# Graph attention on one core: q of two tiles by seven half-width products, with the bias laid into the PSUM bank

## The chip, the cores and the metric

The kernel runs on one core of a Trainium2 chip. The metric is the device time of one execution in microseconds; before the change it is 1974.93 us, the median of three runs (1974.34 to 1975.01). The profile is of one further execution, with a span of 1981.3 us and a granted TensorE clock of 0.990. Engines are named as in the profile: PE is TensorE, PEld its weight loads, DVE VectorE, ACT ScalarE, POOL GpSimd, SP SyncE.

## The reference

The input x is 16 batches of 1024 rows of 512 numbers, and adj a 1024 x 1024 matrix of zeros and ones, sparse and denser towards its first rows and columns. All is fp32.

```python
q = (x @ Wq + bq).reshape(b, n, 8, 64)
k = (x @ Wk + bk).reshape(b, n, 8, 64)
v = (x @ Wv + bv).reshape(b, n, 8, 64)
scores = jnp.einsum('bqhd,bkhd->bhqk', q, k) / jnp.sqrt(64.)
scores = scores + (1.0 - adj) * -1000000000.0
attn = softmax(scores)
out = jnp.einsum('bhqk,bkhd->bqhd', attn, v).reshape(b, n, 512) @ Wo + bo
result = layernorm(x + out)
```

## The kernel before

The kernel makes lists of the neighbours from adj once (DVE, in the first 200 us). Then it does two things at a time. The "fronts" transpose x and compute q, k and v, two tiles of 128 rows (a pair) at a time, and store them in DRAM. The "blocks" gather rows of q, k and v by the lists (POOL), multiply and sum them to scores (DVE), take exponentials and weigh v (ACT, part DVE), and add up (DVE, PE). A finished tile goes through the output projection (po) and the norm. The program is emitted in steps, one for each of 560 blocks and a lead-in of 34: in each step the engines get a block's work, and PE gets units of front or output work for a share of time in credit. What a unit leaves in PSUM is emptied in the next step (`later(1, ...)`).

PSUM has eight banks: a ring of four for short-lived results, one each for x and z, two for sums.

```python
def fill_psum(name):
    return psum.tile([P, HALF], F32, tag="fill", name=name, bufs=4)
```

k and v of a pair come from seven products of blocks (two rows of tiles times k and v together), with weights combined once at the start (T1 to T4) and x combined per pair (s1 to s4). q is computed plainly, four products of 128x128x512 for each tile, and gets scale and bias when DVE takes it out of its bank:

```python
def product(name, lhs, w, out):
    def unit(c):
        if c == 0:
            PS[name] = fill_psum(name)
        p = PS[name]
        nc.tensor.matmul(p, lhs()[:, ts(c, P)], w[:, c, :], start=(c == 0), stop=(c == NPAIR - 1))
        if c == NPAIR - 1:
            del PS[name]
            later(1, lambda: out(p))
    return [(PRODUCT, lambda c=c: unit(c), None) for c in range(NPAIR)]
# ... in pair(b, j):
def out_q(i, p):
    q = work.tile([P, D], F32, tag="q", name=f"q_{b}_{tt[i]}", bufs=2)
    nc.vector.scalar_tensor_tensor(q, p, scale, bq_bc, op0=OP.mult, op1=OP.add)
    later(1, lambda: nc.sync.dma_start(q_rows[b % ROWS][ds(tt[i] * P, P), :], q))
# ...
units = []
units += unit("x", lambda: a(0, 0), B11, True, out_e, None)
units += unit("p6", s(2), T2, True, out_w, None)
units += q0
units += unit("x", lambda: a(0, 1), B21, False, lambda: out_k(0, R["x"]), "e")
units += unit("p7", s(3), T3, True, out_g, None)
units += xt
units += unit("z", s(1), T1, True, out_v1, None)
units += q1
units += unit("p4", lambda: a(1, 1), T4, True, out_k1, None)
units += unit("z", s(4), B22, False, out_v0, "v1")
```

A unit of k and v is two products of 128x128x512. Units p6, p7 and p4, the products of q and po, and the transposes pxT (of x) and poT (of an attention result) each take a bank of the ring of four; x and z have their own.

The transposes of x, and the combinations of two tiles after them:

```python
def out():
    XT[b, t] = work.tile([P, D], F32, tag="xT", name=f"xT_{b}_{t}", bufs=4)
    nc.scalar.copy(XT[b, t], p)
    # ...
    if t % 2 and (b, t) != (0, 1):
        later(1, combine)

def combine():
    s = [work.tile([P, HD2], F32, tag=f"s{i}", name=f"s{i}_{b}_{t}", bufs=1 + i // 4) for i in (1, 2, 3, 4)]
    x0, x1 = XT[b, t - 1], XT[b, t]
    nc.vector.tensor_tensor(s[0], x1[:, 0:HD2], x1[:, HD2:D], op=OP.add)
    # ... three more of 128x256
```

The exponential, and the order in a step (cut):

```python
nc.scalar.activation(PV[n][:, D:], S.pop(n), AF.Exp, bias=bias)
# ... a step n:
exponentials(n + 3)              # ACT
products(n + 4)                  # DVE: qk
gather(...)                      # POOL, up to AHEAD = 8 blocks ahead (AHEAD_LAST = 11 without fronts)
weigh(n + 1)                     # DVE, for some blocks
add_own(n); scores(n + 4)        # DVE
normalise(...)                   # DVE, at the end of a tile
for fn in plan.pop(n, ()): fn()  # what later(...) has put off: PSUM is emptied here
weigh(n + 2)                     # ACT, eight of 128x64, for most blocks
for fn in rest.pop(n, ()): fn()
add_up(n)                        # PE, for blocks of a list
# ... then units of PE, until the credit of this step is used up
```

## Time and profile before

| what | value |
|---|---|
| time, median of 3 runs | 1974.93 us |
| span of the profiled execution | 1981.3 us |
| PE busy | 1914.7 us (97%) |
| DVE busy | 1786.6 us (90%) |
| ACT busy | 1554.5 us (78%) |
| products that read wq (q), 1024 records | 481.5 us |
| DVE taking q out of PSUM, 128 operations of 128x512 | 87.2 us |
| 16 DMA engines, mean | 284 GB/s |

Busy time is the time in which an engine has at least one instruction under way. The rows of instructions that follow each other overlap, so the mean length of one is more than the time it takes of its engine; the distance from start to start is that time. A matmul in fp32 shows as two records. "Idle before" a group is what the engine waited ahead of it, and the releaser is what ended the wait.

### The profile page before, as it was taken

Reading aid. Unit: us, or ns where it says so; the run is one execution under the profiler, and the core shown is the slowest. Engines: PE = TensorE matmul, PEld = TensorE weight load, DVE = VectorE, ACT = ScalarE, POOL = GpSimd, SP = SyncE. Lnnn points to the kernel's source line nnn. Section 1 sums busy time; section 2 is a strip of 40 time slices with the busy share of each in tenths; the row PEclk is TensorE's granted clock in tenths of the full one; section 3 lists DMA queues with packets and bytes.
Section 4 is the critical chain, followed back from the end, with each engine's and each line's share of the span. In section 5 each row is a group of like instructions: output and inputs, shape, how many; then the busy total and the mean of one; then the engine's idle time right before and its main releaser. Section 6 shows DMA issues by size and latency. Waiting matters only on the chain.

```text
span 1981.3 us, 25750 instructions
## 1 busy us (share of the span) xinstructions
PE 1914.7 (97%) x5375; PEld 923.3 (47%) x5375; DVE 1786.6 (90%) x3756; ACT 1554.5 (78%) x6096; POOL 1288.2 (65%) x1206
## 2 busy tenths in 40 slices
PE   8988999999999999999999999999999999999895
PEld 3434454444545454454544445454444545444442
DVE  2789999999899999999998999989899999999895
ACT  3525878878797887879888787879789798978785
POOL 1653565756667676767667586766757675566684
PEclk9999999999999999999999999999999999999998
DMA  6697887888879788888889788888978889998994
GB/s 250 214 339 253 265 303 246 301 280 273 315 262 318 253 303 287 299 296 270 306 255 319 269 290 285 298 303 262 312 260 290 293 291 321 313 316 269 324 313 154
DMA packets 191140, 563.10 MB, mean 284 GB/s; under 512 B 31711, under 2 KB 31739, under 8 KB 190974
## 3 DMA queue, kind: packets, MB, share of 16 engines
q0 software_dynamic: 121632, 403.22, 61.9%
q1 hardware_dynamic: 66736, 153.16, 20.9%
q10 hardware_dynamic: 2606, 4.99, 0.7%
q14 instruction: 122, 1.00, 0.2%
q8 instruction: 44, 0.72, 0.1%
HBM read 442.25 MB, written 143.71 MB: 296 GB/s over the span
## 4 chain that ended last, share of the span: by engine, by line
PE 75%; DVE 12%; issue 3%; ACT 2%; DMA 0%; POOL 0%; another core or an unknown queue 0%; DVEq 0%; POOLq 0%; ACTq 0%
PE po L584 19%; PE pq L584 17%; PE pp L698 13%; PE z L698 9%; PE x L698 9%; DVE qk L931 3%; DVE s L935 2%; PE poT L1008 2%; PE pxT L555 2%; PE sum L981 2%; PE sum L980 2%; ACT pv L955 1%; DVE pv L971 1%; PE pm L646 1%; DVE o L1000 1%
## 5 line engine op out<-in xcount | busy, mean ns | idle before, releaser
L910 POOL DMA_INDIRECT kvg<-kv_rows,key_row x560 | 629.5, 1124 | 435.0 <-ACT pv L945 111.6
L955 ACT ACTIVATE pv<-kvg,pv 128x64 f32<-128x64 f32 x3552 | 894.4, 338 | 0.0
L584 PE MATMUL pq<-wq,xT 128*128 128x512 f32 x1024 | 481.5, 600 | 2.0 <-issue 1.5
L584 PE MATMUL po<-wo,oT 128*128 128x512 f32 x944 | 436.7, 595 | 4.2 <-DVE y L804 1.9
L935 DVE TENSOR_REDUCE s<-qk 128x8 f32<-128x512 f32 x560 | 380.8, 680 | 6.0
L931 DVE TENSOR_TENSOR qk<-qt,kvg 128x512 f32<-128x512 f32 x464 | 317.4, 684 | 4.8 <-DMA kvg<-kv_rows,key_row 3.1
L584 PEld LDWEIGHTS pq<-wq,xT 128*128 128x128 f32 x1024 | 192.7, 193 | 223.2 <-issue 209.4
L584 PEld LDWEIGHTS po<-wo,oT 128*128 128x128 f32 x944 | 175.5, 191 | 206.1 <-issue 190.8
L698 PE MATMUL pp<-t,s 128*128 128x512 f32 x504 | 239.6, 598 | 9.5 <-DVE s L570 9.5
L698 PE MATMUL x<-b,xT 128*128 128x512 f32 x504 | 237.1, 593 | 0.0
L971 DVE TENSOR_TENSOR pv<-pv,pv 128x520 f32<-128x520 f32 x336 | 232.9, 693 | 0.0
L945 ACT ACTIVATE pv<-s,absent 128x8 f32<-128x8 f32 x464 | 135.3, 293 | 107.7 <-DVE s L935 69.2
L830 POOL DMA_INDIRECT out_dram<-y,asked_row x128 | 153.2, 1197 | 37.6 <-issue 26.1
L894 POOL DMA_INDIRECT qt<-q_rows,asked_row x128 | 139.8, 1092 | 36.8 <-issue 35.0
L594 ACT ACTIVATE sq_k<-kv 128x128 f32<-128x128 f32 x512 | 150.6, 299 | 10.0 <-DVE kv L721 9.0
L698 PEld LDWEIGHTS pp<-t,s 128*128 128x128 f32 x504 | 95.2, 191 | 119.1 <-issue 107.7
L698 PEld LDWEIGHTS x<-b,xT 128*128 128x128 f32 x504 | 94.6, 190 | 112.4 <-issue 109.0
L752 POOL DMA_INDIRECT y<-in_x_dram,asked_row x102 | 116.0, 1137 | 30.6 <-issue 30.0
L904 POOL DMA_INDIRECT qg<-q_rows,query_row x96 | 106.1, 1105 | 27.2 <-issue 25.3
L698 PE MATMUL z<-b,s 128*128 128x512 f32 x252 | 118.5, 592 | 0.7 <-DVE kv L726 0.7
L698 PE MATMUL pp<-t,xT 128*128 128x512 f32 x252 | 118.5, 593 | 0.1
L698 PE MATMUL z<-t,s 128*128 128x512 f32 x252 | 118.6, 593 | 0.0
(195 smaller groups left out, 2608.8 us busy)
## 6 DMA issues: line engine op xcount, KB each, us to landing
kv_rows<-kv SPq DMA_DIRECT2D x128, 512.0 KB
x<-in_x_dram SPq DMA_DIRECT2D x128, 256.0 KB
q_rows<-q SPq DMA_DIRECT2D x128, 256.0 KB
kvg<-kv_rows,key_row POOLq DMA_INDIRECT x560
residual<-y_sorted SPq DMA_DIRECT2D x26, 256.0 KB
y<-residual SPq DMA_DIRECT2D x26, 256.0 KB
adj<-in_adj_dram POOLq DMA_DIRECT2D x8, 512.0 KB
spill<-oT SPq DMA_DIRECT2D x10, 256.0 KB
```

The lines of the kernel that those rows point to most:

```text
L584: nc.tensor.matmul(p, lhs()[:, ts(c, P)], w[:, c, :], start=(c == 0), stop=(c == NPAIR - 1))
L594: nc.scalar.activation(sq, s[:, ts(h, P)], AF.Square, scale=scale, accum_out=sums[:, h:h + 1])
L698: nc.tensor.matmul(R[bank], l[:, ts(c, P)], right[:, c, :], start=(first and c == 0), stop=(c == 1), skip_group_check=True,)
L752: nc.gpsimd.indirect_dma_start(out=y, out_offset=None, in_=x_rows, in_offset=bass.IndirectOffsetOnAxis(ap=asked_row[:, t:t + 1], axis=0), ...
L830: nc.gpsimd.indirect_dma_start(out=out_rows[b, t], out_offset=bass.IndirectOffsetOnAxis(ap=asked_row[:, t:t + 1], axis=0), in_=y, in_offse ...
L894: nc.gpsimd.indirect_dma_start(out=QT[b, t], out_offset=None, in_=q_rows[b % ROWS], in_offset=bass.IndirectOffsetOnAxis(ap=asked_row[:, t: ...
L910: nc.gpsimd.indirect_dma_start(out=KG[n], out_offset=None, in_=kv_rows[b % ROWS], in_offset=bass.IndirectOffsetOnAxis(ap=key_row[:, g:g + ...
L931: nc.vector.tensor_tensor(QK[n], q, KG[n][:, 0:D], op=OP.mult)
L935: nc.vector.tensor_reduce(S[n], QK.pop(n).rearrange("p (h d) -> p h d", d=HD), axis=AX.X, op=OP.add)
L945: nc.scalar.activation(PV[n][:, D:], S.pop(n), AF.Exp, bias=bias)
L955: nc.scalar.activation(pv[:, ts(h, HD)], v[:, ds(D + h * HD, HD)], AF.Copy, scale=pv[:, D + h:D + h + 1])
L971: nc.vector.tensor_tensor(PV[b, t], PV[b, t], pv, op=OP.add)
```

## The change

q of a pair is now computed by seven block products instead of eight, in the same scheme as k and v: the two tiles are the block rows, the halves of the 512 numbers the block columns, and Wq is taken as four blocks A11, A12, A21, A22 of 256x256. One product of blocks is two products of 128x128x256. It uses the combinations s1 to s4 of x that k and v have already, and combinations U1 to U4 of Wq made once at the start (U1 in the place of A12). It is for TensorE: a pair has fourteen half-width products in place of eight full ones.

A bank of PSUM of its own ("xq") holds the two halves of the sums. ACT fills it with the bias ahead of a pair (`prefill`), and the products add to that; the bias of the right half is stored as a difference to the left. The ring "fill" goes from four banks to three for it. Three products (q6, q7, q4) go to banks of the ring. DVE adds the parts in five operations of 128x256, ACT copies two.

The scale leaves q and its bias and goes into the exponential. To make room in SBUF, the rings of y and kv lose a buffer each. The lists at the start are begun a step apart (`EDGES_FROM`), with more PE work beside them (`LISTS_SHARE`); the sorting of residuals moves by three steps, and the look-ahead of gathers in the last stretch (`AHEAD_LAST`) falls from 11 to 9. The combinations of x for the next pair wait until the product that reads s1 has been issued.

```diff
-KG_BUFS, Q_BUFS, PV_BUFS, Y_BUFS = 8, 7, 5, 6
+KG_BUFS, Q_BUFS, PV_BUFS, Y_BUFS = 8, 7, 5, 5
-SORTED_AT = range(-16, -3)
-AHEAD_LAST = 11
+SORTED_AT = range(-13, 0)
+AHEAD_LAST = 9
-EDGES_FROM = (-17, -16, -15, -13, -11, -8, -7, -18)
+EDGES_FROM = (-17, -16, -15, -14, -13, -12, -11, -18)
-LISTS_SHARE = 4.6
+LISTS_SHARE = 5.4
@@
-            return psum.tile([P, HALF], F32, tag="fill", name=name, bufs=4)
+            return psum.tile([P, HALF], F32, tag="fill", name=name, bufs=3)
@@
+        A11, A12, A21, A22 = (W["q"][:, ts(i, 2), ts(j, HD2)] for i in range(2) for j in range(2))
+        U2, U3, U4 = (one.tile([P, 2, HD2], F32, name=name) for name in ("u2", "u3", "u4"))
+        U1, mixed = A12, [False]
@@ combine
+                    if (b, t) != (0, 3) and last_s.get((b * NT + t) // 2 - 1) is None:
+                        later(1, combine)
+                        return
@@ pair
+            L, RIGHT = slice(0, HD2), slice(HD2, D)
+            def prefill():
+                R["xq"] = q_psum(f"xq_{b}_{j}")
+                nc.scalar.copy(R["xq"], bq_bc)
+            def q_unit(bank, left, right, after, need=None):
+                def pe():
+                    if bank in (L, RIGHT):
+                        out, first = R["xq"][:, bank], False
+                    else:
+                        R[bank] = out = fill_psum(f"{bank}_{b}_{j}")[:, L]
+                        first = True
+                    l = left()
+                    for c in range(2):
+                        nc.tensor.matmul(
+                            out, l[:, ts(c, P)], right[:, c, :], start=(first and c == 0), stop=(c == 1),
+                            skip_group_check=True,
+                        )
+                    later(1, after)
+            # q_e, q_11: ACT copies of 128x256; q_w, q_g, q_22, q_21, q_12: DVE adds of 128x256
             units = []
             units += unit("x", lambda: a(0, 0), B11, True, out_e, None)
+            units += [(0.0, prefill, lambda: mixed[0] and before_this in q_done)]
             units += unit("p6", s(2), T2, True, out_w, None)
-            units += q0
+            units += q_unit(L, lambda: a(0, 0), A11, q_e)
             units += unit("x", lambda: a(0, 1), B21, False, lambda: out_k(0, R["x"]), "e")
+            units += q_unit("q6", s(2), U2, q_w, "qe")
             units += unit("p7", s(3), T3, True, out_g, None)
+            units += q_unit(L, lambda: a(0, 1), A21, q_11, "qe")
             units += xt
             units += unit("z", s(1), T1, True, out_v1, None)
-            units += q1
+            units += q_unit("q7", s(3), U3, q_g)
+            units += q_unit(RIGHT, s(1), U1, q_22)
             units += unit("p4", lambda: a(1, 1), T4, True, out_k1, None)
+            units += q_unit("q4", lambda: a(1, 1), U4, q_21, "q22")
             units += unit("z", s(4), B22, False, out_v0, "v1")
+            units += q_unit(RIGHT, s(4), A22, q_12, "q22")
@@ gather, without fronts: kv ring of 4 instead of 5; load_y: at most 4 tiles instead of 5
@@ exponentials
-            nc.scalar.activation(PV[n][:, D:], S.pop(n), AF.Exp, bias=bias)
+            nc.scalar.activation(PV[n][:, D:], S.pop(n), AF.Exp, bias=bias, scale=scale)
```

## The prediction

> **What bounds the kernel now.** I read the page's busy shares first, then the same busy times cut into stretches, then the groups by shape, and last the timelines. The page says that TensorE (PE) is busy nearly throughout:
>
> ```profile
> PE 1914.7 (97%) x5375; PEld 923.3 (47%) x5375; DVE 1786.6 (90%) x3756; ACT 1554.5 (78%) x6096; POOL 1288.2 (65%) x1206
> ```
>
> A share over the whole span mixes stages, so here is the busy time by stretch (from, to, length; then PE, weight loads, DVE, ACT and POOL busy in us, and the PE clock). The first three lines are of one cut, the last is of a finer one:
>
> ```profile
> 300.00:1600.00 1300.00, 1294.15 (x3671) 627.72 (x3671) 1213.78 (x2491) 1078.57 (x4288) 898.42 (x826) 1.00 0.85 286
> ...
> 0.00:200.00 200.00, 177.58 (x477) 82.80 (x478) 140.14 (x347) 89.82 (x290) 84.33 (x98) 0.97 0.77 265
> 1700.00:1982.00 282.00, 243.64 (x666) 116.00 (x665) 245.86 (x552) 220.07 (x843) 181.13 (x167) 0.95 0.81 280
> ```
>
> ```profile
> 1700.00:1800.00 100.00, 90.86 (x260) 43.80 (x260) 98.14 (x185) 85.45 (x358) 60.99 (x55) 0.98 0.89 306
> ```
>
> From 300 to 1600 us PE is busy for 1294 of 1300 us. PE alone sets that time, with DVE close behind at 93.4% and ACT at 83%. From 1700 on it is DVE that is full (98.1%) and PE waits. So a saving of PE time counts before about 1700 us, and not after.
>
> The chain that ended last gives the same picture (PE 75% of it). The list of waits names what PE itself waited for, in us in total, times, and the longest:
>
> ```profile
> PE poT L1008 <- DVE o L1000: 10.6, 7, 3.2
> PE pp L698 <- DVE s L570: 9.5, 3, 4.0
> ...
> PE po L584 <- DVE y L804: 1.9, 1, 1.9
> PE po L584 <- DVE g L717: 1.2, 2, 1.0
> ```
>
> The last two are waits for a PSUM bank of the "fill" ring to be emptied. There are hardly any with four banks.
>
> **What an instruction costs.** A busy PE or DVE row overlaps the next one, so I take the pitch, start to start. The PE timeline:
>
> ```profile
> 361.25 2.74 PE L584 MATMUL po<-wo,oT 128*128 128x512 f32 x6
> 363.82 0.59 PE L980 MATMUL sum<-pv,sums 128*128 128x256 f32 x2
> 364.26 0.61 PE L981 MATMUL sum<-pv,sums 128*128 128x264 f32 x2
> 364.70 1.02 PE L584 MATMUL po<-wo,oT 128*128 128x512 f32 x2
> 365.56 3.60 PE L584 MATMUL pq<-wq,xT 128*128 128x512 f32 x8
> 368.99 1.88 PE L698 MATMUL x<-b,xT 128*128 128x512 f32 x4
> ```
>
> Each product is two records. Four 128x128x512 products take 368.99 - 365.56 = 3.43 us, so one takes 0.858. A 256-wide one takes 364.26 - 363.82 = 0.44, half of that: narrow products lose next to nothing in this kernel. The DVE timeline:
>
> ```profile
> 361.35 0.69 DVE L959 TENSOR_TENSOR pv<-kvg,pv 128x512 f32<-128x512 f32 x1
> 361.95 0.69 DVE L971 TENSOR_TENSOR pv<-pv,pv 128x520 f32<-128x520 f32 x1
> ...
> 382.00 0.42 DVE L568 TENSOR_TENSOR s<-xT 128x256 f32<-128x256 f32 x1
> 382.33 0.42 DVE L569 TENSOR_TENSOR s<-xT,xT 128x256 f32<-128x256 f32 x1
> 382.67 0.42 DVE L570 TENSOR_TENSOR s<-s,xT 128x256 f32<-128x256 f32 x1
> ```
>
> A 512-wide operation has a pitch of 0.60 us, a 256-wide one 0.33 to 0.34. On ACT, two 512-wide copies out of PSUM at 380.74 let the next instruction start at 381.68, so 0.47 to 0.48 each.
>
> **What the Trainium skill says.** (1) "TensorE: Matmul & The Clock Gate", section "Back-to-back issue gap": the spacing of matmuls is set by the weight load and the matmul together. The trace agrees that this doesn't bite yet: a load lasts 0.19 us, a 256-wide record streams for 0.215. The margin is thin, as the new products have no 512-wide neighbours in a run of four records. (2) "Perfetto Trace Analysis", section "Optimizing Scalar/DVE Operations": each DVE or ACT operation carries an overhead of its own, and part of its profiled latency overlaps the next. The trace agrees: 0.68 us long at a pitch of 0.60, and two halves of 0.34 cost more than one whole. (3) The same page, section "Matmuls": independent groups should rotate through PSUM banks so that emptying one overlaps the next group. The change takes one bank out of that rotation. (4) "PSUM — Partial Sum Buffer", section "PSUM bank collisions raise a hardware error": two engines may not be in one bank at once, even at different columns. Both halves of q now share one bank, so emptying one half excludes writing the other. Nothing in the trace before shows this.
>
> **The change part by part.** Counting the records that read wq by stretch and dividing by 16 (two tiles, four products, two records) gives the pairs of tiles: 11.6 before 300 us (one of them plain, which stays as it is), 43.7 from 300 to 1600, 4.1 from 1600 to 1700, 4.9 after. A pair in the middle takes 1300 / 43.7 = 29.7 us.
>
> PE: eight 512-wide products, 8 x 0.858 = 6.86 us a pair, become fourteen 256-wide ones, 14 x 0.43 = 6.01. It saves 0.86 us a pair. For 63 pairs that is 54 us; the 58.4 pairs before 1700 give 50, and this is the most that can arrive.
>
> DVE: out go two 512-wide operations (2 x 0.60 = 1.20), in come five 256-wide ones (5 x 0.34 = 1.70): 0.50 us more a pair. From 300 to 1600 that is 22 us, on 1213.8: 1235.7. PE falls there to 1294 - 37.5 = 1256.7. So DVE would stand at 1235.7 / 1262.5 = 97.9%, as full as it was at its fullest (98.1%). The 4.9 pairs after 1700 cost 2.5 us more, as DVE sets the time there.
>
> ACT: a 512-wide fill of the bank with the bias (0.48) and two 256-wide copies (0.28 each, an estimate between the 0.25 pitch of its 128x64 operations and 0.48) are 1.04 us a pair. ACT goes to (1078.6 + 45) / 1262.5 = 89%. It executes in order, and eight weighing operations (2.0 us) stand ahead of the fill in most steps. PE has one x and one p6 unit, 3.4 us, to cover the way from the last read of the bank, over the fill, to the next product.
>
> The scale in the exponential and the unscaled bias cost nothing: the exponential already runs, with one more constant. The smaller y and kv rings and the shorter look-ahead of the last stretch free the memory for the new weight combinations; I allow no time for them beyond the width of the range. The lists brought together and the larger share of PE work beside them can win back a little of the 22 us that PE idles before 200 us; I put 3.
>
> Banks: per batch of four pairs the fill ring serves 4 x 7 + 16 = 44 allocations before and 4 x 8 + 16 = 48 after. A bank may be held 4 x 119 / 44 = 10.8 us on average before, and 3 x 115 / 48 = 7.2 after. In the timeline a pq bank begun at 1026.27 is read at 1030.48 and free at 1031.2 (4.9 us), so the mean suffices, but not bursts: at 1024.1 a po bank (begun 1019.8, free at 1025.7), a poT bank and two pxT banks are held at once. With three, the second pxT would have waited until 1025.7, some 1.5 us.
>
> The sum: -50 (PE before 1700) + 2.5 (DVE after) - 3 (start) + L, where L is what PE loses to banks, to the bias fill and to a DVE without slack. For L I choose 0.35 us a pair, 20 us: one burst like that in every fourth or fifth pair. The net is -30, so 1975 - 30 = 1945 us.
>
> **Rivals.** A: the PE saving arrives whole, L near zero, about 1926. For it: PE hardly ever waited with DVE at 93%, and DVE ran at 98% later without breaking down. Against it: three things are tightened at once (DVE slack, banks, ACT order). B: DVE takes over as the bound. It needs 1235.7 / 0.98 = 1261 us for the middle, which is 39 us less than now, so DVE alone can't eat the gain; with the usual idle of 6.6% it would need 1323 and the kernel would be 20 us slower than before. For it: ACT and DVE wait for each other (a DVE wait of 2.65 us for the ACT square at 379.5). Against it: most of DVE's idle waits are for PE, which go as PE gets faster. C: the missing bank makes PE wait in nearly every pair, 0.9 us or more. Then nothing is left, 1970 to 1985. For it: the burst above; against it: the new order puts units that use no bank of the ring behind both transposes.
>
> **Range and chances.** L between 5 and 45 us, and some 5 us either way for start and end, give 1927 to 1972 as the range for 8 in 10. More than 2% faster is under 1935.4, so L under about 10: 0.26. More than 2% slower (over 2014) needs a loss of 90 us, which only a broken rhythm of all three engines brings: 0.04. The rest, 0.70, lies within 2%.
>
> **What would show it right or wrong.** Right: the q products read as fourteen 256-wide products at a pitch of 0.43 us, PE busy is down by about 50 us, DVE is at 96 to 98% from 300 to 1600, and PE has new waits, for DVE evacuations or for the ACT fill, of some 20 us in all. Wrong: a pitch above 0.45 for the new products (weight loads no longer hidden); PE waits above 45 us (C); PE still at 99.5% in the middle (A); or a start or end stretch that moved by more than 10 us.

## The result, and the profile after

The changed kernel takes 2074.2 us (median of four runs, 2073.18 to 2075.94), the kernel before 1974.64 us (median of four). The ratio is 1.0505, with a 95% interval of 1.0487 to 1.0523: about 100 us slower, where 30 us faster was predicted. The profiled execution has a span of 2071.3 us and a granted TensorE clock of 0.982 (before: 1981.3 and 0.990).

The busy times of the page after, in us:

```profile
PE 1898.7 (92%) x6131; PEld 1069.6 (52%) x6131; DVE 1826.6 (88%) x3949; ACT 1629.0 (79%) x6285; POOL 1288.0 (62%) x1206
```

PE has fallen from 97% to 92%, and no other engine has taken its place: DVE has gone from 90% to 88%. The chain that ended last says the same more sharply. It was 75% PE before; its first line after:

```profile
PE 8%; DVE 6%; ACT 4%; issue 2%; DMA 1%; POOL 1%; SPq 0%; POOLq 0%; DVEq 0%; ACTq 0%
```

The pieces of the chain that the profile could follow add up to some 22% of the span, so the chain has broken up. I take from it no more than that PE no longer forms it.

The busy times by stretch (from, to, length; PE, weight loads, DVE, ACT, POOL; PE clock, DMA share, GB/s):

```profile
300.00:1600.00 1300.00, 1231.37 (x4048) 700.13 (x4047) 1196.29 (x2532) 1093.29 (x4274) 868.26 (x802) 1.00 0.82 278
0.00:200.00 200.00, 160.95 (x489) 89.11 (x490) 126.47 (x325) 77.96 (x232) 71.85 (x85) 0.93 0.66 227
1700.00:2072.00 372.00, 315.26 (x974) 171.89 (x972) 320.11 (x709) 290.32 (x1116) 223.06 (x206) 0.95 0.81 273
```

In the middle PE was busy for 1294 of 1300 us, and now 1231. DVE is at 92.0% (before 93.4%), ACT at 84.1% (83.0%), GB/s fell from 286 to 278. No engine is full. In the first 200 us PE has lost 17 us of busy time. In the last stretch DVE is at 86% (before 87%, 245.86 of 282 us; the 98.1% shown above was of 1700 to 1800 us alone).

What PE waited for (us in total, times, longest):

```profile
PE xq L780 <- ACT xq L769: 56.9, 39, 5.0
PE pxT L570 <- DVE q L798: 17.1, 10, 6.1
PE poT L1108 <- DVE kv L747: 8.9, 4, 3.8
PE poT L1108 <- DVE o L1100: 7.8, 4, 4.1
PE pxT L570 <- DMA x<-in_x_dram: 6.9, 2, 3.5
PE pxT L570 <- ACT oT L1112: 6.9, 5, 3.5
```

The first line is the bank of the q sums: the first product of a pair waits for ACT's fill with the bias. The second, third and sixth are units that take a bank of the ring of three and wait until an earlier one has been emptied; the others wait for their inputs. Before, the longest line of a wait for a bank stood at 1.9 us (the 10.6 us of poT were for its input o), and the fill did not exist.

In the stretch from 300 to 1600 us the first line is:

```profile
PE xq L780 <- ACT xq L769: 34.0, 23, 3.1
```

PE's idle times of over 0.15 us add up to 68 us there. Sorted by what the named releaser set free, 34 us are for the bank of q and 34 for a bank of the ring. Before, the sum was 5.6 us, of which 2.7 were for the ring.

Was the saving there at all? The groups of the new products, by shape:

```profile
L780 PE MATMUL xq<-wq,xT 128*128 128x256 f32 x504 | 136.5, 394 | 56.9 <-ACT xq L769 56.9
L780 PE MATMUL q<-u,s 128*128 128x256 f32 x504 | 131.9, 385 | 7.1 <-ACT xT L574 4.4 <-ACT oT L1112 2.6
L780 PE MATMUL xq<-wq,s 128*128 128x256 f32 x504 | 129.5, 380 | 0.0
L780 PE MATMUL q<-u,xT 128*128 128x256 f32 x252 | 66.0, 385 | 2.8 <-DVE q L804 2.8
```

1764 records are fourteen products for each of 63 pairs, two records each. The busy times add up to 463.9 us, which looks like little against the 481.5 before, but a busy time counts the tail of each record that the next one overlaps. Start to start, two such records of one unit lie 0.216 us apart (the median), 0.43 us a product as predicted.

Because of this overlap I did the accounting from the starts of PE's records. Each record has an ideal: 0.429 us for a width of 512 (half of the 0.858 us of a product), in proportion for others. What the distance to the next start has beyond it is a "wait" where the trace shows PE idle for over 0.15 us, and "slower" otherwise (a lower granted clock is in this part). The 560 blocks are counted by their score reductions on DVE. All in us:

| stage | kernel | length | ideal of PE | waits | slower | DVE not idle | ACT not idle |
|---|---|---|---|---|---|---|---|
| to block 70 | before | 394.8 | 352.7 | 24.7 | 13.3 | | |
| | after | 421.8 | 341.5 | 53.7 | 22.4 | | |
| blocks 70 to 455 | before | 1259.0 | 1248.3 | 2.2 | 8.1 | 1178.3 | 1043.0 |
| | after | 1307.0 | 1210.5 | 75.9 | 19.2 | 1201.2 | 1094.5 |
| from block 455 | before | 327.4 | 277.6 | 25.4 | 7.4 | | |
| | after | 342.5 | 272.4 | 39.8 | 13.3 | | |

(The small rest of a length is time before the first or behind the last product of the stage.) PE's own work fell by 11.2 + 37.8 + 5.2 = 54.2 us. PE's waits rose by 117.1 us, and 26.1 us more went into slower records. That is +89 of the 90 us between the two spans; by stage +27, +48 and +15. (The medians lie 100 us apart, since the profiled execution before took 1983.14 us, 8 us more than its median; so the loss in the accounting is some 10 us low.)

One case of the wait for the bank of q, in the timeline of all engines (start, length, then the instruction; in brackets the idle time before it and its releaser):

```profile
1023.45 1.88 PE L724 MATMUL pp<-t,s 128*128 128x512 f32 x4
...
1024.13 2.02 ACT L1055 ACTIVATE pv<-kvg,pv 128x64 f32<-128x64 f32 x8
1024.14 1.41 DVE L667 TENSOR_TENSOR vsum<-vsum,kv 128x512 f32<-128x512 f32 x2
...
1025.47 0.42 DVE L819 TENSOR_TENSOR q<-xq,q 128x256 f32<-128x256 f32 x1
...
1026.05 0.57 ACT L769 COPY xq<-bq_bc 128x512 f32<-128x512 f32 x1
...
1026.68 1.13 PE L780 MATMUL xq<-wq,xT 128*128 128x256 f32 x4 [1.35 <-ACT xq L769]
```

The last product of the pair before had ended at 1021.9. DVE reads it only at 1025.47, 3.6 us later: it stands in the next step, behind the normalisation of a tile and two additions to vsum. ACT fills the bank behind that and behind its own weighing (1024.13, 2.02 us long), and PE, whose x and p6 units had ended at 1025.33, has stood for 1.35 us. Over the pairs 11 to 56 the way takes on average 3.85 us from the product to DVE's read, 1.5 us from there to the fill, and 1.4 us to the product, of which PE stands still for 0.80 us.

### The profile page after: what moved, and what is told of

Its sections match the earlier page's. It is cut to its first block, busy times and chain, and to the rows that moved or that the text cites. A ratio compares the mean times of both kernels' runs of the same rounds, so it can differ in the third digit from the quotient of the medians.

```text
span 2071.3 us, 27903 instructions
## 1 busy us (share of the span) xinstructions
PE 1898.7 (92%) x6131; PEld 1069.6 (52%) x6131; DVE 1826.6 (88%) x3949; ACT 1629.0 (79%) x6285; POOL 1288.0 (62%) x1206
## 3 DMA queue, kind: packets, MB, share of 16 engines
q14 instruction: 127, 1.04, 0.1%
## 5 line engine op out<-in xcount | busy, mean ns | idle before, releaser
L724 PE MATMUL x<-b,xT 128*128 128x512 f32 x504 | 242.0, 603 | 1.5 <-ACT e L737 1.5
L780 PE MATMUL xq<-wq,xT 128*128 128x256 f32 x504 | 136.5, 394 | 56.9 <-ACT xq L769 56.9
L780 PEld LDWEIGHTS xq<-wq,xT 128*128 128x128 f32 x504 | 93.2, 192 | 131.4 <-ACT xq L769 91.1
L780 PE MATMUL q<-u,s 128*128 128x256 f32 x504 | 131.9, 385 | 7.1 <-ACT xT L574 4.4
L724 PEld LDWEIGHTS x<-b,xT 128*128 128x128 f32 x504 | 95.9, 194 | 75.7 <-issue 67.1
L780 PEld LDWEIGHTS q<-u,s 128*128 128x128 f32 x504 | 96.1, 193 | 72.4 <-issue 44.1
L780 PE MATMUL xq<-wq,s 128*128 128x256 f32 x504 | 129.5, 380 | 0.0
L724 PE MATMUL z<-t,s 128*128 128x512 f32 x252 | 124.6, 619 | 0.0
```

The lines of the kernel that those rows point to most:

```text
L724: nc.tensor.matmul(R[bank], l[:, ts(c, P)], right[:, c, :], start=(first and c == 0), stop=(c == 1), skip_group_check=True,)
L780: nc.tensor.matmul(out, l[:, ts(c, P)], right[:, c, :], start=(first and c == 0), stop=(c == 1), skip_group_check=True,)
```

## The experiments

Every time is given as the ratio to the kernel before on the same chip, with its 95% interval, since the kernel before took between 1973.8 and 1987.2 us on the chips used. The changed kernel itself has its 1.0505 from a chip of its own, so a difference below half a per cent between chips is read as none; runs on one chip are compared more finely. The changed kernel was not timed again beside its variants: where one of them stands somewhat above 1.0505 (e2, e7, e8), this shows that it gained nothing, and not that it lost. "Middle waits" are PE's waits from block 70 to 455 in the accounting above (before 2.2, after 75.9 us).

The theories at the outset: the fill on ACT (F); the ring of three banks (T); ACT's order, in which the copy q_11 must wait for DVE's q_w (A); the order at the start (S); DVE without slack (D).

### Without the fill: e1

The bias is not filled in, and so it is missing from q; the first product of a pair starts the bank.

```diff
                 R["xq"] = q_psum(f"xq_{b}_{j}")
-                nc.scalar.copy(R["xq"], bq_bc)
...
-                        out, first = R["xq"][:, bank], False
+                        out, first = R["xq"][:, bank], "begun" not in R
+                        R["begun"] = True
```

> The changed kernel without the ACT fill of the xq bank: the first product of a pair starts the bank afresh, and the bias of q is left out. Theory F (the one xq bank is passed on serially, from the last DVE read over the ACT fill to PE, and PE waits there): the 57 us of PE waits for the fill go or shrink to what the DVE read alone costs, and the time falls by 25 to 55 us, to 2020 to 2050. Theory N (the ring of three banks is what costs): the fill is not to blame, the waits move to other products, 2062 to 2078.

Measured: 1.0526 (1.0494 to 1.0558), no gain; middle waits 82.6. PE's longest wait:

```profile
PE xq L780 <- DVE q L819: 32.6, 17, 5.1
```

PE now waits at the same place for DVE's last read of the bank instead of the fill behind it. F falls as far as the fill itself goes: it is the name that the profile gives, and the late read stands behind it.

### The lists begun as before: e2

```diff
-SORTED_AT = range(-13, 0)
+SORTED_AT = range(-16, -3)
-EDGES_FROM = (-17, -16, -15, -14, -13, -12, -11, -18)
+EDGES_FROM = (-17, -16, -15, -13, -11, -8, -7, -18)
-LISTS_SHARE = 5.4
+LISTS_SHARE = 4.6
```

> The changed kernel with the start as it was before: EDGES_FROM, SORTED_AT and LISTS_SHARE at their old values. Theory S (the lists a step apart fill DVE in one stretch and hold up all that stands behind them, 35 us until the first block): 2035 to 2050. Rival (the start is late because the emptying of q's banks now sits between DVE and ACT, whatever the lists' order): within 8 us of 2074.

Measured: 1.0614 (1.0568 to 1.0661). Block 0 starts at 157.1 us instead of 179.1 (before the change: 143.8), but block 35 at 303.6 and 307.2: the lead is spent at once. S falls as the cause; on the same chip this run is 0.9% slower than e1 and e3, so the new constants seem to do the changed kernel some good.

### The last product of q ahead of z: e3

```diff
-            units += unit("z", s(4), B22, False, out_v0, "v1")
             units += q_unit(RIGHT, s(4), A22, q_12, "q22")
+            units += unit("z", s(4), B22, False, out_v0, "v1")
```

> The changed kernel with the last product of q (right half, s4) ahead of the last z unit instead of behind it, so that DVE and ACT have one more unit of 1.7 us to free and fill the xq bank. Nothing is left out. Theory F: the PE waits for the fill fall from 57 to under 20 us, and the time to 2025 to 2050. Theory N: 2065 to 2078.

Measured: 1.0524 (1.0495 to 1.0554), middle waits 90.5: no gain. From the product to DVE's read it is 3.28 us instead of 3.85, but from there to the fill 3.68 instead of 1.5: the fill stays where ACT's step has it. This run moved only half of what it was to move; e9 does the rest.

### Three banks in the kernel before: e4

The kernel before, with nothing changed but the ring.

```diff
-            return psum.tile([P, HALF], F32, tag="fill", name=name, bufs=4)
+            return psum.tile([P, HALF], F32, tag="fill", name=name, bufs=3)
```

> The kernel before with its ring cut from four PSUM banks to three, one bank left unused, and nothing else changed. Theory N: most of the loss of the middle, 35 us or more, shows here too, 2005 or more. Theory F: three banks suffice but for bursts, 1977 to 1992.

Measured: 1.0287 (1.026 to 1.0313), 2045.41 us: the missing bank alone costs 58 us on that chip, at an unchanged amount of work. The middle of this run and PE's four longest waits there:

```profile
300.00:1600.00 1300.00, 1261.59 (x3536) 605.49 (x3535) 1173.49 (x2401) 1043.72 (x4144) 864.83 (x802) 1.00 0.83 276
```

```profile
PE pxT L555 <- DVE g L717: 7.2, 5, 4.3
PE po L584 <- ACT xT L559: 4.4, 5, 1.3
PE poT L1008 <- DVE q L614: 3.1, 4, 1.8
PE poT L1008 <- DVE w L714: 3.0, 2, 1.7
```

PE has gone from 1294 to 1262 us here. All four lines are waits for a bank of the ring. No line is large; the loss lies in 37 short waits, 32 us in sum, for whichever bank was last. The middle waits are 35.3 (before 2.2), and the stage to block 70 is 14 us longer. T stands. The 58 us are two fifths of what PE lost in the changed kernel (117 us of waits and 26 of slower records).

### The other parts of the change, in the kernel before: e5, e6, e10, e11

e5 gives the kernel before the smaller memory of the changed one: a y and a kv buffer less, one load of y less ahead, the look-ahead of the last stretch of 9, and the rows of adj in the larger ring.

```diff
-KG_BUFS, Q_BUFS, PV_BUFS, Y_BUFS = 8, 7, 5, 6
+KG_BUFS, Q_BUFS, PV_BUFS, Y_BUFS = 8, 7, 5, 5
-AHEAD_LAST = 11
+AHEAD_LAST = 9
...   # every ring "kv": bufs=5
+     # bufs=4
-            tag, bufs = ("kvg", KG_BUFS) if J > 16 else ("kv", 5)
+            tag, bufs = ("kvg", KG_BUFS)
-    ... sum(b * NT + t not in SPILL for b, t in Y) < 5:
+    ... sum(b * NT + t not in SPILL for b, t in Y) < 4:
```

> The kernel before with only the smaller rings of the change: y 5 instead of 6, kv 4 instead of 5, at most 4 tiles of y loaded, AHEAD_LAST 9, the rows of adj in the kvg ring. Theory M (memory: the smaller rings cost a good part of the 100 us): ratio to before 1.010 or more. Theory P (PSUM: it is the banks and q's chain in them): ratio 0.998 to 1.006.

Measured: 0.9991 (0.9978 to 1.0005). The memory costs nothing.

e6 is e5 with the changed kernel's constants for the lists (the diff of e2 the other way round).

> The same, with the start of the change on top (EDGES_FROM, SORTED_AT, LISTS_SHARE); q is still computed plainly, with four banks. Theory S (the new order of the start costs by itself): 1.010 to 1.020 above the run with small rings alone. Theory P: within 0.004 of it, as PE makes up for a late start.

Measured: 1.0056 (1.0035 to 1.0078): 0.6% slower. To block 70 it is faster (382.2 us, against 389.0 in e5), but its middle is 1275.5 against 1260.9. That is more than the 0.004 over e5 that theory P allowed and less than theory S asked for. It is a small part of the loss at most, and in the changed kernel e2 points the other way.

e10 adds to e5 the engine work of the change, with nothing that waits for it: for each pair two DVE additions of 128x256 and two ACT copies of 128x512.

```diff
                 nc.vector.scalar_tensor_tensor(q, p, scale, bq_bc, op0=OP.mult, op1=OP.add)
                 later(1, lambda: nc.sync.dma_start(q_rows[b % ROWS][ds(tt[i] * P, P), :], q))
+                extra = work.tile([P, HD2], F32, tag="extra", ...)
+                nc.vector.tensor_tensor(extra, bq_bc[:, 0:HD2], bq_bc[:, HD2:], op=OP.add)
+                extra2 = work.tile([P, D], F32, tag="extra2", ...)
+                nc.scalar.copy(extra2, bq_bc)
```

> The kernel before, with the small rings, and for each pair two more DVE additions of 128x256 and two more ACT copies of 128x512 that nothing waits for (about 0.68 us of DVE and 0.96 of ACT a pair, as much as the change adds). Plain q, four banks. Theory L: the load alone makes PE wait, ratio 1.015 or more. Theory F or banks: DVE and ACT take it in their idle time, ratio 0.998 to 1.008.

Measured: 1.0077 (1.006 to 1.0093), with nothing of it in the middle, which stays at 1260.5 us with 3.8 us of waits:

```profile
300.00:1600.00 1300.00, 1293.30 (x3658) 626.21 (x3657) 1237.43 (x2573) 1119.04 (x4367) 912.81 (x825) 1.00 0.85 285
```

DVE stands at 95.2% and ACT at 86.1%, both fuller than in the changed kernel, and PE is busy for 1293 of 1300 us. So full engines alone do not make PE wait, as long as there are four banks and PE has its old amount of work.

e11 is e10 with the ring of three banks (the diff of e4).

> The same with the ring cut to three banks. Additive: 1.029 (three banks) plus what the load costs alone. Theory L with banks (a ring of three passes every delay of DVE on to PE, so that the two multiply): 1.045 or more, and 6 us or more of PE waits a batch, as in the changed kernel. Theory F: 1.028 to 1.036.

Measured: 1.0343 (1.0324 to 1.0363). The bank and the load add up (0.029 + 0.008); they do not multiply. This goes against theory L, in which the load would make the missing bank much dearer. The waits for the ring from 300 to 1600 us are 34 us here, as in the changed kernel. The 0.016 between this and the changed kernel, and the 54 us of PE work that the changed kernel has less, must come from something that only the changed kernel has.

### An own place for q_e: e8

The copy q_e goes to the other q tile, so that the copy q_11 need not wait for q_w to have read it.

```diff
-                nc.scalar.copy(new_q(0)[:, L], R["xq"][:, L])
+                nc.scalar.copy(new_q(1)[:, L], R["xq"][:, L])
+                new_q(0)
...
-                nc.vector.tensor_tensor(q[:, RIGHT], R["q6"], q[:, L], op=OP.add)
+                nc.vector.tensor_tensor(q[:, RIGHT], R["q6"], R["q", 1][:, L], op=OP.add)
```

> The changed kernel with the first ACT copy of q (e) into the other tile of the pair, so that the second ACT copy (q_11) no longer has to wait until DVE has read e. Nothing is left out. Theory A (ACT, which executes in order, is held by that copy behind a late DVE, and all that ACT empties is held with it): 20 us or more faster than the changed kernel, ratio 1.03 to 1.041, the most of it at the start. Theory P: ratio 1.043 to 1.052.

It was tried for this place in the start of the changed kernel, where an ACT copy waits 11 us for DVE, which is at work on a list:

```profile
140.34 0.37 ACT L801 COPY q<-xq 128x256 f32<-128x256 f32 x1 [11.01 <-DVE q L798]
```

Measured: 1.0613 (1.0554 to 1.0672); to block 70 it takes 415.1 us instead of 421.8, but the middle waits are 92.8. A falls as a cause of the loss in the middle.

### Four banks by letting x and z share one: e7

```diff
-            return psum.tile([P, HALF], F32, tag="fill", name=name, bufs=3)
+            return psum.tile([P, HALF], F32, tag="fill", name=name, bufs=4)
...
-                            [P, HALF], F32, tag=bank, name=f"{bank}_{b}_{j}", bufs=1
+                            [P, HALF], F32, tag="xz", name=f"{bank}_{b}_{j}", bufs=1
...   # p6 ahead of x, z(s4) ahead of q4
```

> The changed kernel with its ring back at four banks: x and z, which are never needed at the same time in a new order of units (p6 ahead of x, the last z ahead of q4), share one bank. Nothing is left out. Theory P: the 1.029 that three banks cost by themselves comes back, and the ratio to before falls from 1.0505 to 1.015 to 1.03; the waits of pxT and poT for a bank go. Rival D (DVE and ACT are simply too late, and PE waits for them at the next place whatever the banks): ratio 1.04 or more, with the waits moved to x, z and xq.

Measured: 1.0598 (1.0562 to 1.0633). PE's longest waits:

```profile
PE xq L780 <- ACT xq L769: 45.9, 24, 5.1
PE pp L724 <- DVE s L588: 24.6, 15, 7.6
```

The waits for the ring are nearly gone, but the order that the shared bank needed puts p6 first in a pair, and p6 waits for the combinations of x. The run tells nothing clean about the fourth bank; e13 does that better.

### The fill at once: e9

e3, with the fill for the next pair emitted straight behind the last read of the bank instead of with the next pair's units.

```diff
                 q_done[b, j] = True
+                if b * NT // 2 + j + 1 < B * NT // 2:
+                    fill_for(b * NT // 2 + j + 1)
```

> The changed kernel with the last product of q ahead of the last z unit, and with the ACT fill of the next pair's xq bank emitted straight behind the DVE operation that reads the bank last (in the runs before it stood at the end of ACT's step, behind eight weighings, and came 1.5 to 3.7 us after that read). Nothing is left out. Theory F (the serial way over the xq bank costs PE its time): the waits for the fill fall from 57 us below 15, the waits of a batch from 6.9 to about 4 us, the ratio to 1.02 to 1.038. Theory L (DVE and ACT have no slack any more; a wait removed comes back elsewhere): ratio 1.042 or more.

Measured: 1.0553 (1.0535 to 1.0571), middle waits 75.7. PE hardly waits for the fill any more, but in the same amount elsewhere:

```profile
PE x L724 <- ACT e L737: 28.2, 21, 3.8
PE pxT L570 <- DVE q L804: 20.2, 12, 6.1
```

What ACT waited for explains it. First the changed kernel, then e9:

```profile
ACT xq L769 <- DVE q L819: 62.1, 35, 7.9
```

```profile
ACT xq L769 <- DVE q L825: 243.0, 61, 13.8
```

The fill now stands ahead of the weighing in ACT's order, and ACT stands still for it: 243 us in 61 pairs, 4 us each. All that comes behind it on ACT, the emptying of x among it, comes later. Whether ACT or PE waits for DVE's late read is a choice of order; the lateness is not.

### Less DVE work ahead of that read: e12

The changed kernel without six of the seven additions to vsum of a batch (the mean of v is then incomplete). They take 0.60 us each, 0.9 us a pair, and many stand just ahead of DVE's last read, as in the timeline above.

```diff
-                    for v in kv:
-                        nc.vector.tensor_tensor(VSUM[b], VSUM[b], v, op=OP.add)
+                    pass
```

> The changed kernel without six of the eight DVE additions of a batch that sum v for rows without neighbours (the sum is then of the first pair alone): 3.6 us less DVE a batch, more than the 2 us that the change adds. Theory L: the PE waits of a batch fall from 6.9 by 3 us or more, ratio 1.025 or less. Theory F: ratio 1.04 or more.

Measured: 1.0374 (1.0357 to 1.0391), middle waits 57.5. It has two readings that this run cannot part: DVE has 40 us less work in the middle, and the way from the last product to DVE's read is 3.26 us instead of 3.85. The ratio lies between the two forecasts. From 300 to 1600 us, the waits for the ring fell from 34 us to 25 and those for the bank of q from 34 to 30, so most of the gain is not on the way over the bank of q: with less to do, DVE empties the banks of the ring sooner as well. Together with e10, where more work alone cost nothing in the middle, this suggests that DVE's load counts where banks are short; this is argued, not shown.

### The fourth bank, freed from the sums: e13, e14, e15, e16

The sums of a list take one bank instead of two; the denominators of the lists are left out for it, and only the tile's own part is taken. The freed bank goes to the ring. The one-bank sums were not run by themselves; DVE's time in the middle is the same with them (1199.8 us in e13, 1201.2 in the changed kernel).

```diff
-            ... tag="fill", name=name, bufs=3)
+            ... tag="fill", name=name, bufs=4)
-                PSUM[b, t] = psum.tile([P, 2, HALF], F32, tag="sum", ...)
+                PSUM[b, t] = psum.tile([P, HALF], F32, tag="sum", ...)
...
-            nc.tensor.matmul(PSUM[b, t][:, 0, 0:HD2], m, pv[:, 0:HD2], **kw)
-            nc.tensor.matmul(PSUM[b, t][:, 1, 0:HD2 + HEADS], m, pv[:, HD2:], **kw)
+            nc.tensor.matmul(PSUM[b, t][:, 0:HD2], m, pv[:, 0:HD2], start=(i == 0), **kw)
+            nc.tensor.matmul(PSUM[b, t][:, HD2:], m, pv[:, HD2:D], start=False, **kw)
```

> The changed kernel with a ring of four banks and its order of units untouched: the sums of the lists take one bank instead of two, and the eight columns of their denominators are left out (the output is normalised wrongly; all other work stays). Additive: the 33 us that three banks cost between block 70 and 455 come back there, waits of 76 fall to about 43, ratio 1.025 to 1.036. If the xq bank or the missing margin of DVE is what holds PE: waits of 65 or more, moved to xq, ratio 1.04 or more.

Measured: 1.043 (1.0379 to 1.048), middle waits 64.7. PE's longest waits from 300 to 1600 us:

```profile
PE xq L780 <- ACT xq L769: 36.6, 20, 3.9
PE xq L780 <- issue: 6.9, 5, 2.7
```

The waits for the ring have gone from 34 us to 4, and all those for the bank of q have risen from 34 to 50. The fourth bank brings some 0.8%, hardly clear of the noise, and not the 2.9% that it was worth in the kernel before. That refutes the additive theory: in the changed kernel, the bank of q then holds PE back in its place.

e14 adds the fill at once (the diff of e9, with the order of e3):

> The same with the last product of q ahead of the last z and the fill straight behind the last read (as in e9). Additive with the xq chain at 20 us: ratio 1.010 to 1.025, waits below 30. If only the margin matters: no better than e13.

Measured: 1.0498 (1.0463 to 1.0533), some half a per cent slower than e13 on the same chip; ACT waits 212.0 us for the last read, as in e9.

e15 is e14 with the lighter DVE of e12, e16 is e13 with it:

> All three: four banks, early fill, and six of eight additions of v a batch left out on DVE. All causes named are then removed; the waits between block 70 and 455 should be below 15 and the saving of PE work show at last: ratio 0.985 to 1.008. If it stays at 1.02 or more, a cause is still missing.

> Four banks and the lighter DVE, the fill where the change has it. If the xq chain costs 20 us on its own: waits of 20 to 30 between block 70 and 455, ratio 1.008 to 1.022. If the chain only waits because DVE is late: as e15.

Measured: e15 1.0453 (1.0425 to 1.0481), e16 1.0248 (1.0223 to 1.0272). With the fill at its old place the lighter DVE brings 0.018 and the middle waits go from 64.7 to 49.1; with the fill ahead it brings only 0.0045, which is not clear of the noise. PE's longest waits in e16 from 300 to 1600 us:

```profile
PE xq L779 <- ACT xq L768: 26.5, 20, 2.6
PE xq L779 <- issue: 8.5, 6, 2.7
```

With the smaller lines of xq, 44 of 51 us are waits for the bank of q. So with four banks and less on DVE, the hand-over of the one bank of q is nearly all that is left.

### Two banks for q: e17, e18

The bank freed in e13 becomes a second bank of q, so that a pair fills one while the other is still to be read; the ring stays at three. The condition that holds back the fill looks two pairs back instead of one.

```diff
-            return psum.tile([P, HALF], F32, tag="xq", name=name, bufs=1)
+            return psum.tile([P, HALF], F32, tag="xq", name=name, bufs=2)
...
-            before_this = (b, j - 1) if j else (b - 1, NT // 2 - 1)
+            before_this = divmod(max(b * NT // 2 + j - 2, 0), NT // 2)
...   # the sums of a list in one bank, as in e13
```

> The changed kernel with the bank that the sums of the lists give up (their denominators are left out) used as a second xq bank; the ring stays at three. The fill of a pair no longer waits for the last read of the pair before. If the single xq bank costs PE time of its own: its waits (38 us from block 70 to 455) go and do not come back, waits 35 to 50 there, ratio 1.020 to 1.036. If they only move: waits of 60 or more, ratio 1.04 or more.

Measured: 1.0363 (1.0346 to 1.038), middle waits 63.9. PE's longest waits:

```profile
PE xq L780 <- ACT xq L769: 31.4, 25, 3.3
PE pxT L570 <- DVE q L798: 15.9, 12, 6.1
```

The hand-over costs PE 0.45 us a pair instead of 0.80. The fill no longer has to wait for DVE's read, but it is still emitted with the pair that uses it and so stands behind ACT's weighing of that step. From 300 to 1600 us the waits for the bank of q fall from 34 us to 21, and those for the ring stay (34 and 37). So the one bank of q is a cause of its own beside the ring, of some 1.4%.

e18 adds the lighter DVE:

> The same with six of eight additions of v a batch left out on DVE. If bank and DVE add up: 10 to 18 us of waits less than e17 from block 70 to 455, ratio 1.005 to 1.022.

Measured: 1.0248 (1.023 to 1.0267), 2023.65 us, middle waits 49.1. The lighter DVE takes 11 us from the waits for the ring (37 to 26, from 300 to 1600 us) and nothing from those for the bank of q (21 and 21). No version came near the kernel before. Two runs that might have gone further were not made: four banks in the ring and two for q at once, and the second bank of q with its fill emitted a unit earlier.

### The runs side by side

The last two columns are PE's idle times of over 0.15 us from 300 to 1600 us, summed from the trace by what the named releaser set free.

| run | what | ratio | middle, us | middle waits, us | at the bank of q, us | at the ring, us |
|---|---|---|---|---|---|---|
| after | the change | 1.0505 | 1307.0 | 75.9 | 34 | 34 |
| e4 | before, three banks | 1.0287 | 1298.7 | 35.3 | - | 32 |
| e10 | before, more load | 1.0077 | 1260.5 | 3.8 | - | 3 |
| e11 | before, both | 1.0343 | 1301.0 | 36.9 | - | 34 |
| e9 | after, fill at once | 1.0553 | 1316.3 | 75.7 | 6 | 49 |
| e12 | after, lighter DVE | 1.0374 | 1291.5 | 57.5 | 30 | 25 |
| e13 | after, four banks | 1.0430 | 1301.8 | 64.7 | 50 | 4 |
| e16 | after, four banks, lighter DVE | 1.0248 | 1282.6 | 49.1 | 44 | 7 |
| e17 | after, two q banks | 1.0363 | 1292.0 | 63.9 | 21 | 37 |
| e18 | after, two q banks, lighter DVE | 1.0248 | 1280.0 | 49.1 | 21 | 26 |

The kernel before has 3 us at the ring. Three banks of the ring bring 32 to 34 us, in the old kernel as in the changed one; the one bank of q brings 34 more. Where the ring gets its fourth bank, PE waits at the bank of q instead.

## Why the prediction was wrong

**The work of the engines: right.** PE was to save 54 us in all: 54.2. The pitch of 0.43 us a product came as read off the narrow products before, and the weight loads stay hidden. DVE was to have 0.50 us more a pair: 22.9 us over the 44 pairs of the middle, 0.52. ACT was to have 1.04: 51.5 / 44 = 1.17. The sign that I had named for the first, PE's busy time down by about 50 us, was a poor one: it fell by 16 us, because the 26 us of slower records count as busy, and so do the tails of records that PE waits behind, which are counted at their full length of some 0.38 us and not at their pitch (some 11 us more of them: the waits rose by 117 us, PE's idle time by 106).

**L: the step that failed.** "For L I choose 0.35 us a pair, 20 us: one burst like that in every fourth or fifth pair." It measured (117.1 + 26.1) / 63 = 2.3 us a pair, of which 1.9 are waits and 0.4 slower records. The sum of the prediction with the measured L reads -54 + 117 + 26 = +89 us. L was not mis-sized for one reason. Two are shown, a third is argued:

1. *The bank of the ring.* I compared how long a bank may be held on average (7.2 us) with how long one is (4.9 us), found room, and counted bursts from one look at the timeline. e4 measured it: 58 us / 63 = 0.92 us a pair. That is rival C, "0.9 us or more" a pair, in size. I put it aside because the new order has units without a ring bank behind the transposes; they did not help enough, since the waits for the ring are about the same in the changed kernel (34 us from 300 to 1600 us) as in e4 (32), which has the old order. A fourth bank gives only 0.8% back in e13 and 1.3% between e12 and e16, as PE then waits at the bank of q. The Trainium skill's "Perfetto Trace Analysis", section "Optimization Strategy" under "Identifying Performance Opportunities", says that the same gap repeating on the engine that should be saturated can mean that there isn't enough SBUF or PSUM for the next tile. The two halves of that come apart here: less SBUF cost nothing (e5), one PSUM bank 2.9%.

2. *The bank of q.* I took "one x and one p6 unit, 3.4 us" as what covers the way from the last read over the fill to the next product. But the way begins with the last product, since DVE's read of it is put off to the next step: 3.85 + 1.5 + 1.4 = 6.8 us on average. The prediction named the waiting of ACT behind its weighing, and left out the 3.85 us before it. e17 shows this hand-over as a cause apart from the ring (34 us to 21 at the bank of q); e1 and e9 show that leaving the fill out or putting it forward does not help, as DVE's read is as late as ever. The other worry about this bank, that the emptying of one half keeps PE from the other, shows no wait in the changed kernel: all 56.9 us stand at the first product of a pair.

3. *The distance between the engines.* Rival B was put aside with "DVE alone can't eat the gain", since DVE's work, 1236 us, fits into 1261. It does fit: DVE never became full (92.0% where 97.9% was predicted), and e10 shows that a fuller DVE alone costs PE nothing. In the middle PE had 1248 us of its own work against 1178 of DVE's before, 70 us more; after it 1210.5 stands against 1201.2, 9 us more. It is tempting to call this lost lead the cause, but the runs speak against it as a cause by itself: e10 has a lead of some 45 us (DVE 1204) and 3.8 us of middle waits, while e16, with four banks in the ring too, has one of some 50 us (DVE 1161) and 49.1. A lighter DVE wins 1.2 to 1.8% (e12, e16, e18). So DVE's load makes the waits for short banks longer; how much of the loss this is has not been shown.

The three don't add up to separate numbers. Where one is taken away, part of its waits come back at the next: the fourth bank is worth 2.9% before and about 1% after, and the lighter DVE 0.45% with the fill put forward and 1.8% without. The 49 us of middle waits that e16 and e18 still have lie at the bank of q in e16 (44 of 51 us of idle time from 300 to 1600 us), and about half at each in e18 (21 and 26 of 48). What remains open is whether both banks together would bring the saving of PE work through, as no version has both.

**Start and end: wrong in sign.** The start was to win 3 us, and lost 27 to block 70: PE's work fell by 11 there, its waits rose by 29. Part of it is in the changed kernel's PE timeline at 140 us, where a transpose finds the three banks taken while DVE works through a list:

```profile
133.58 0.66 PE L570 MATMUL pxT<-ident,x 128*128 128x128 f32 x4 [1.43 <-DVE w L740]
140.31 1.12 PE L570 MATMUL pxT<-ident,x 128*128 128x128 f32 x4 [6.08 <-DVE q L798]
```

DVE empties three products of q for a pair where it emptied two, and any one of them can stand behind a list here. e4, with three banks alone, loses 14 us to block 70, about half of the 27. The order of the lists is not it (e2); the other half stays open. At the end DVE was to remain the bound, at a cost of 2.5 us. That was read off one stretch of 100 us: from 1700 us to the end DVE stood at 87% before and at 86% after, so it was not the bound throughout in either. The stage lost 15 us, as PE's waits there rose too (25.4 to 39.8).

**The slower records.** I had no term for them: 26 us. The granted clock went from 0.990 to 0.982, and to 0.93 in the first 200 us (0.97 before), where PE waits most. The Trainium skill's "Perfetto Trace Analysis", section "Matmul Optimizations", says that the matmul engine scales its power with its use and that matmuls should be issued back to back; the two clocks agree with that in direction. No run here sets the clock apart from the waits.

**The range.** It put L between 5 and 45 us and gave 4% to a loss of 90, "which only a broken rhythm of all three engines brings". That sentence comes near to what happened. But the three things that I had listed as "tightened at once" against rival A were treated as three small risks, one of which might cost a burst now and then. Two of them, the ring and the hand-over of q's bank from PE over DVE and ACT to PE, each came to half of the waits in the middle.

## What to carry to other kernels

Work saved on the bounding engine arrives only if the results can still be handed on in time: here 54 us of saved work were outweighed by 117 us of waits at two places where banks are short, while no other engine was full. A bank taken from a ring that a saturated engine rotates through is best tried by itself on the old kernel (one line, 2.9% here), and a buffer that goes around through several engines is to be counted from the last write to the next write, with the waiting for a turn in each engine's order (6.8 us here, of which the operations themselves are 1 us). When a wait's named releaser is removed and the time stays, look at what that releaser was waiting for.

## What the runs showed that I had not expected

- Narrow products cost in proportion to their width: 0.216 us from start to start for a record of 128x128x256 against 0.429 for 512, also in runs of four records with other shapes around them.
- An instruction placed early on an engine that works in order is dear: the same fill waited 62 us in all behind its DVE read at its old place and 243 us when put forward (e9), and the kernel was no faster although PE's wait for it had gone.
- One PSUM bank of eight was worth 2.9% in a kernel whose PE was busy for 97%, with no single line of waits over 10 us in total to show for it.
- DVE at 95% and ACT at 86% left PE at 1293 of 1300 us (e10); DVE at 92% and ACT at 84% in the changed kernel left it at 1231. An engine's share did not tell which of them held PE back.
